# Cross-attention with layer norm: first input block in rows of 2 KB, keys by input block, third tile's transpose later

## The chip, the cores and the metric

The kernel runs on one core of a Trainium2 chip. The metric is the device time of one execution in microseconds (us). The runs of the kernel before give a median of 541.96 us.

The names of the engines are those of the profile: PE is TensorE (matmuls; PEld its weight loads), DVE is VectorE, ACT is ScalarE, POOL is GpSimd, and SP is SyncE, which here only issues DMAs.

## The reference, cut to what matters

Sixteen heads of 32 channels attend from 4 x 2048 rows of `x` (512 channels) to 77 rows of context per batch. The result goes through an output projection, the input is added, and a layer norm follows.

```python
qs = (q @ wq)   # q = x, split into 16 heads of 32
ks = (k @ wk)   # k = ctx_1024, 77 rows per batch
vs = (v @ wv)   # v = ctx_1024
scores = einsum('bhqd,bhkd->bhqk', qs, ks) / sqrt(32)
scores = where(mask, -inf, scores)
attn = einsum('bhqk,bhkd->bhqd', softmax(scores), vs)
out = attn.reshape(B, L, 512) @ wo + q
return (out - mean(out)) / sqrt(var(out) + 1e-5) * gamma + beta
```

## The kernel before

**Tiles, blocks and groups.** The 8192 rows are cut into 64 tiles of 128 rows. Two tiles make a block (32 blocks), and four tiles a group (16 groups), which is what one load of the transposed input `xT` brings. Every projection is done in three matmuls per 128 input channels: each operand is split into a rounded part and a rest (ACT copies the rounded part, DVE or POOL subtracts), and rounded x rounded, rounded x rest and rest x rounded are added up in PSUM. The 512 input channels are four such input blocks, called c = 0 to 3 below.

**What one tile goes through.**

- `q_visit` (L154): the query projection, one quarter of the output channels of a group at a time, into one PSUM bank; `q_evac` (L171) copies it to SBUF on DVE.
- `scores` (L277): 16 small matmuls into four PSUM banks.
- `maxima` (L291): 16 DVE instructions, which add the mask, take the row maximum and write the scores to `pbuf[t % 3]`. The first four heads empty the first bank, and so on.
- `exps` (L305): 16 ACT instructions. `recip` (L316) on DVE, then `normalise` (L321) on POOL.
- `transp` (L345): DVE transposes the 128 x 1280 probabilities in 32 x 32 squares into the tile `B`, of which one holds the two tiles of a block.
- `regroup` (L357): when both tiles of a block are transposed, SP issues 12 DMAs, which carry `B` to `PT`.
- `av` (L375): attention x values, for a block; `av_hi` (ACT, L406) and `av_lo` (DVE, L410) split the result; `o_proj` (L430) is the output projection; then residual, moments and scale.

**Order.** Nothing is reordered by a scheduler: each engine runs its instructions in the order in which the program issues them. A loop runs over u = 0, 2, 4, ... and issues the work of tiles u and u + 1 together with older stages of earlier tiles; the last 16 tiles follow a list written out by hand (`ORDER`), which the change doesn't touch. Two PSUM facts matter: there are eight banks in all, and a matmul into a new bank waits until the bank's last reader is done.

**The buffer of B.** `B` has two buffers. At the start they hold `ctx_f` and `ctx_h` (the context and its rounded part). `B_0` (tiles 0 and 1) takes the place of `ctx_f`. `ctx_h` is read until the value projections of batches 2 and 3 (L215, issued at u = 4), so `B_1` (tiles 2 and 3) takes the buffer of `B_0`. The first transpose into `B_1`, `transp(2)`, therefore waits until all 12 DMAs of `regroup(0)` have read `B_0`. In the loop body of u = 2 it is issued after `maxima(3)` and `values_evac`, and ahead of `split_wo(2)`, `split_wo(3)` (L246), `recip(3)` and, in the body of u = 4, `maxima(4)`.

**The start.** Ten matmuls on a zero tile (L499, `pw`) keep PE busy from the first microsecond. Meanwhile SP issues in turn a quarter of the first 256 rows of `xT` (128 KB in rows of 1 KB, L507) and a quarter of `wq` (256 KB in rows of 2 KB, L508), four times; then the context (L510), `wk` (L512, loaded into `stage_a` and split into `woh` and `wol`, whose buffers serve `wo` later), the mask, and the second 256 rows of the group (L515). Eight semaphores go round over SP's DMAs, so that a DMA is issued only when the one eight places before it has landed. For each c, ACT and DVE split the piece of `xT` and of `wq` (L125, L126) and PE runs 12 matmuls for tiles 0 and 1 (L523). Then the keys follow (L180), into four banks, one for each quarter m of the output channels:

```python
for m in range(NG):
    keys_part(pks, m, (0, 1))
for m in range(NG):
    keys_part(pks, m, (2, 3))
```

`keys_part(pks, m, cs)` runs three matmuls for each c of `cs`: with `woh`, with `woh` and the context's rest, and with `wol`. So the first quarter asks for c = 1 after three matmuls. Behind the keys come `q_visit(0, 0)` for the second 256 rows and `scores(0)`.

Of the kernel before, what the change touches and what calls it, by code (L numbers as in the profile page):

```python
# [17 lines left out]
P = 128  # L18
# [9 lines left out]
NG = H // GH  # L28
HEADS = [GH * g + j for j in range(GH) for g in range(NG)]
NC_D = D // P  # L30
BLK = 256
GRP = 2 * BLK
MASKED = -3.0e38
EPS = 1.0e-5
WARM = 10
NPB = 3
LAST = 16

# [24 lines left out]
def xattn_layernorm(  # L63
    ctx: ExitStack,
    tc: tile.TileContext,
    x: bass.AP,
    xT: bass.AP,
    ctxT: bass.AP,
    mask: bass.AP,
    wq: bass.AP,  # L70
# [7 lines left out]
    nc = tc.nc  # L78
# [10 lines left out]
    def bank(name):  # L89
        return ps.tile([P, 512], F32, tag="mm", name=name)  # L90
# [20 lines left out]
    stage_a = sb.tile([P, 2, NC_D, D], F32, tag="PT", name="stage_a")  # L111
# [9 lines left out]
    def wview(w, c):  # L121
        return w[c * P : (c + 1) * P, :]

    def split(hi, lo, src):
        nc.scalar.copy(hi, src)  # L125
        nc.vector.tensor_tensor(lo, src, hi.bitcast(F32), ALU.subtract)  # L126
# [4 lines left out]
    fx, gx, qd, qp, bat, pts = {}, {}, {}, {}, {}, {}  # L131
# [44 lines left out]
    def keys_part(pks, m, cs):  # L176
        for c in cs:
            n = 0
            for w, i in ((woh, 0), (woh, 1), (wol, 0)):
                nc.tensor.matmul(  # L180
                    pks[m][:, : NB * (NK + 1)],
                    w[:, c, m * P : (m + 1) * P],
                    ctx_s[c][i][:, :, : NK + 1],
                    start=(c == 0 and n == 0),
                    stop=(c == NC_D - 1 and n == 2),
                )
                n += 1
# [12 lines left out]
    def value_rows():  # L200
        vi = sb.tile([NK2, 2, 32], F32, tag="o", bufs=8, name="vi")
        for q0 in range(0, NK2, 32):
            for a, (z0, z1) in enumerate(((NK, NK2), (NK - TAIL_K, NK))):
                nc.vector.memset(vi[q0 : q0 + 32, a], 1.0)
                lo, hi = max(z0, q0), min(z1, q0 + 32)
                if lo < hi:
                    nc.vector.memset(vi[q0 : q0 + 32, a, lo - q0 : hi - q0], 0.0)
        nc.vector.transpose(vm, vi)
# [128 lines left out]
    def transp(t):  # L337
        b, tt = divmod(t, 2)
        if tt == 0:
            bts[b] = sb.tile([P, 5, 2 * NP * 32], F32, tag="B", name=f"B_{b}")  # L340
        if b < NBLK - 1:
            bt = bts[b].rearrange("p c (q t r) -> p c q t r", q=NP, t=2)[:, :, :, tt, :]
        else:
            bt = bts[b].rearrange("p c (t q r) -> p c q t r", q=NP, t=2)[:, :, :, tt, :]
        nc.vector.transpose(  # L345
            bt.rearrange("p c q r -> p q c r"),
            pbuf[t % NPB].rearrange("p q (c r) -> p q c r", c=5),
        )
# [92 lines left out]
    def moments(t):  # L441
        b, tt = divmod(t, 2)
        st = sb.tile([P, 6], F32, tag="st", bufs=3, name=f"st_{t}")
        nc.vector.bn_stats(st, od[t])
        if tt == 0:
            mvs[b] = sb.tile([P, 2, 2], F32, tag="mv", bufs=3, name=f"mv_{b}")
            rns[b] = sb.tile([P, 2, 2], F32, tag="rn", bufs=3, name=f"rn_{b}")
        mv, rn = mvs[b], rns[b]
        nc.vector.bn_aggr(mv[:, tt, :], st)
        nz = bat[t // TPB][1]  # L450
        if tt == 1:
            k = (t - 1) % TPB
            nc.gpsimd.tensor_tensor(rn[:, 0, :], mv[:, :, 1], nz[:, k : k + 2], ALU.add)
            nc.gpsimd.tensor_tensor(rn[:, 0, :], rn[:, 0, :], mhalf, ALU.pow)
            nc.gpsimd.tensor_tensor(rn[:, 1, :], mv[:, :, 0], rn[:, 0, :], ALU.mult)
            nc.gpsimd.tensor_tensor(rn[:, 1, :], rn[:, 1, :], mneg, ALU.mult)
# [40 lines left out]
    pw = bank("pw")  # L497
    for i in range(WARM):
        nc.tensor.matmul(pw, warm[:, :P], warm, start=True, stop=True)  # L499
# [3 lines left out]
    gx[0] = [sb.tile([P, NC_D, GRP], F32R, tag=t, name=f"{t}_0") for t in ("xth", "xtl")]  # L503
    qd[0] = sb.tile([P, NG, GRP], F32, tag="q", name="q_0")
    x0h, x0l = (a[:, :, :BLK] for a in gx[0])
    for c in range(NC_D):
        nc.sync.dma_start(fx[0, c // 2 * 2][:, c % 2, :BLK], xT[0, :, c, :BLK])  # L507
        nc.sync.dma_start(stage_a[:, 0, c], wview(wq, c))  # L508
    for c in range(0, NC_D, 2):
        nc.sync.dma_start(ctx_f[:, c : c + 2], ctxT[:, c : c + 2])  # L510
    for c in range(NC_D):
        nc.sync.dma_start(stage_a[:, 1, c], wview(wk, c))  # L512
    load_mask(0)
    for c in range(0, NC_D, 2):
        nc.sync.dma_start(fx[0, c][:, :, BLK:], xT[0, :, c : c + 2, BLK:])  # L515
    value_rows()
    pq0 = [bank(f"pq_0_{m}") for m in range(NG)]
    for c in range(NC_D):
        split(x0h[:, c], x0l[:, c], fx[0, c // 2 * 2][:, c % 2, :BLK])
        split(wqh[:, c], wql[:, c], stage_a[:, 0, c])  # L520
        for m in range(NG):
            for n, (w, r) in enumerate(((wqh, x0h), (wqh, x0l), (wql, x0h))):
                nc.tensor.matmul(  # L523
                    pq0[m][:, :BLK],
                    w[:, c, m * P : (m + 1) * P],
                    r[:, c, :],
                    start=(c == 0 and n == 0),
                    stop=(c == NC_D - 1 and n == 2),
                )
# [4 lines left out]
        nc.scalar.copy(qd[0][:, m, :BLK], pq0[m][:, :BLK])  # L534
        nc.vector.tensor_copy(qd[0][:, m + 1, :BLK], pq0[m + 1][:, :BLK])
    pks = [bank(f"pk_{m}") for m in range(NG)]
    for m in range(NG):
        keys_part(pks, m, (0, 1))
    for m in range(NG):
        keys_part(pks, m, (2, 3))  # L540
    for c in range(0, NC_D, 2):
        split(*(a[:, c : c + 2, BLK:] for a in gx[0]), fx[0, c][:, :, BLK:])
    q_visit(0, 0)
    mask_bias(0, slice(0, 1))
    gate(stage_a[:, 1, NC_D - 1, D - 1 :])
# [17 lines left out]
    def pieces(u):  # L563
        return casts.get(u) or [((u + 8) // 4, u % 4)] * (u + 8 < 4 * NGRP)

    evac = [(0, 0)]
    for u in range(0, NT - LAST // 2, 2):
        n = u // 2
        m, k = divmod(u, TPB)

        for q in pieces(u + 2):
            if u >= 4:
                load_xT(*q)
        for t in (u - 4, u - 3):
            if t >= 0:
                load_x(t)
        scores(u)
        maxima(u, 0, H // 2)
        for q in evac:
            q_evac(*q)  # L580
        maxima(u, H // 2, H)
        for q in pieces(u):
            cast_xT(*q)
        exps(u, 0, 3 * H // 4)
        for v in list(vd):
            values_evac(v)
        for q in pieces(u):
            split_xT(*q)
        if u == 0:
            mask_bias(0, slice(1, TPB))  # L590
            split_wv()
        if u >= 6:
            o_proj(u - 6)
        for v in {2: (0,), 4: (2, 3)}.get(u, ()):
            values(v)
        for q in visits(u):
            q_visit(*q)
        if u >= 6:
            residual(u - 6)
            moments(u - 6)  # L600
        if u:
            transp(u - 1)
            regroup(n - 1)
        if u >= 8:
            scale(u - 8)
            scale(u - 7)
        exps(u, 3 * H // 4, H)
        if u >= 8:
            affine(u - 8)
        for q in visits(u):  # L610
            q_evac(*q)
        if u == 0:
            load_wo()
            nc.gpsimd.memset(ident, 0.0)
            nc.gpsimd.affine_select(ident, ident, [[-1, P]], ALU.not_equal, 1.0, base=0, channel_multiplier=1)
        if u == 2:
            split_wo(0)
            split_wo(1)
        if k == TPB - 6 and m + 1 < NB:
            load_mask(m + 1)  # L620
        if k == TPB - 4 and m + 1 < NB:
            mask_bias(m + 1)
        if k == TPB - 2 and m + 1 < NB:
            mask_nan(m + 1)

        scores(u + 1)
        maxima(u + 1, 0, 3 * H // 4)
        recip(u)
        maxima(u + 1, 3 * H // 4, H)
        exps(u + 1, 0, H // 4)  # L630
        normalise(u)
        if u >= 8:
            affine(u - 7)
        for v in list(vd):
            values_evac(v)
        if u >= 4:
            av(n - 2)
            av_hi(n - 2, 0)
            av_hi(n - 2, 1)
        exps(u + 1, H // 4, H)  # L640
        if u >= 5:
            o_proj(u - 5)
        if u >= 4:
            av_lo(n - 2, 0)
        if u >= 5:
            residual(u - 5)
        if u >= 4:
            av_lo(n - 2, 1)
        transp(u)
        for v in {2: (1,)}.get(u, ()):  # L650
            values(v)
        evac = visits(u + 1)
        for q in evac:
            q_visit(*q)
        if u == 2:
            load_xT(*pieces(4)[0])
        if u >= 5:
            moments(u - 5)
        if u == 0:
            mask_nan(0)  # L660
        if u == 2:
            split_wo(2)
            split_wo(3)
        recip(u + 1)
        normalise(u + 1)
        if u >= 8:
            store(u - 8)
            store(u - 7)
# [79 lines left out]
```

## Time and profile before

| | us |
|---|---|
| median of 3 runs | 541.96 |
| lowest and highest run | 539.43, 542.49 |
| the profiled execution | 540.23 |
| its span (first to last instruction) | 538.5 |
| PE busy in the span | 522.8 |
| DVE, ACT, POOL busy | 483.6, 462.6, 404.5 |

The profiled execution took 540.23 us, that is 1.73 us less than the median and inside the spread of the runs; 1.7 us of it lie outside the span. Places in time below are us from the start of the span. In a timeline a row has its start, its duration, engine, line, operation, output<-inputs and shape; in square brackets stands how long the engine had been idle before it and what ended that. In the chain of waits a row is a start, a duration and what the end of the span was waiting for in that time. A list of waits gives the total, how many times and the longest. Matmuls are pipelined, so that rows overlap: a 256-column matmul of the start has a row of 0.28 us, but the next one starts 0.12 us after it.

### The profile page before, as it was taken

To read this page: it belongs to the slowest core of one execution; us is meant where nothing else is said; L and a number is where in the kernel's file an instruction comes from. 1 tells how busy PE (TensorE), PEld (TensorE's weight loads), DVE (VectorE), ACT (ScalarE), POOL (GpSimd) and SP (SyncE) were. 2 spreads that over 40 slices of the span, in tenths; PEclk is the share of its full clock that TensorE was granted. 3 is DMA by queue.
4 is the path that set the end of the run, shared out by engine and by line. 5 is a ranking of instruction groups with operands and counts; after the bars stand their busy time and mean duration, and the time that the engine had idled before them with its cause. 6 is when DMAs were issued, how large, how long until landed. Compare 5 with 4: busy or idle time off the path is not lost.

```text
span 538.5 us, 16101 instructions
## 1 busy us (share of the span) xinstructions
PE 522.8 (97%) x4810; PEld 398.9 (74%) x4810; DVE 483.6 (90%) x2588; ACT 462.6 (86%) x2217; POOL 404.5 (75%) x367
## 2 busy tenths in 40 slices
PE   8999899999999999999999999999999999999795
PEld 5987577777777777777777778777777777766573
DVE  5688899889999898889998998889999988999977
ACT  5687799998899999998899999998899998998410
POOL 0626447888899888888899888888899888856851
PEclk9999999999999999999999999999999999999998
DMA  8934577787777787886777778867777767855854
GB/s 279 401 134 107 160 200 193 211 238 189 191 195 210 214 226 208 225 221 175 193 210 221 209 217 218 235 167 198 210 208 217 216 175 197 236 138 158 255 157 156
DMA packets 59191, 109.96 MB, mean 204 GB/s; under 512 B 9424, under 2 KB 11920, under 8 KB 59104
## 3 DMA queue, kind: packets, MB, share of 16 engines
q1 hardware_dynamic: 56048, 103.10, 68.3%
q0 software_dynamic: 2256, 5.05, 3.4%
q8 instruction: 38, 0.62, 0.5%
q10 hardware_dynamic: 800, 0.79, 0.5%
q14 instruction: 49, 0.40, 0.3%
HBM read 41.79 MB, written 16.78 MB: 109 GB/s over the span
## 4 chain that ended last, share of the span: by engine, by line
PE 76%; DVE 13%; DMA 4%; SPq 2%; ACT 2%; issue 1%; POOL 1%; DVEq 0%; ACTq 0%
PE po L430 29%; PE pq L154 26%; PE sc L277 10%; PE pa L375 9%; DVE pbuf L291 4%; DVE B L345 3%; DMA PT<-B 3%; SPq L357 1%; ACT pbuf L305 1%; PE pk L180 1%; DMA stage_a<-wk 1%; DVE o L486 1%; DVE q L171 1%; DVE AL L410 1%; DVE o L489 1%
## 5 line engine op out<-in xcount | busy, mean ns | idle before, releaser
L305 ACT ACTIVATE pbuf<-pbuf,nm 128x77 f32<-128x77 f32 x1024 | 355.0, 371 | 32.4 <-DVE nm L291 31.1
L305 ACT ACTIVATION_READ_ACCUMULATOR pbuf<-pbuf,nm 128x1 f32 x1024 | 216.4, 211 | 0.0
L321 POOL TENSOR_TENSOR pbuf<-pbuf,ri 128x1232 f32<-128x1232 f32 x63 | 142.3, 2259 | 56.0 <-DVE ri L316 37.2
L291 DVE CUSTOM_DVE_ANT_0 pbuf<-sc,mb 128x77 f32<-128x77 f32 x1024 | 169.2, 231 | 5.5 <-PE sc L277 3.6
L430 PE MATMUL po<-woh,AH 128*128 128x512 f32 x256 | 107.8, 421 | 1.5 <-DVE nm L291 1.5
L345 DVE STREAM_TRANSPOSE B<-pbuf 128x1280 f32<-128x1280 f32 x64 | 95.6, 1494 | 6.5 <-DMA PT<-B 3.5
L430 PE MATMUL po<-wol,AH 128*128 128x512 f32 x256 | 100.3, 392 | 0.0
L430 PE MATMUL po<-woh,AL 128*128 128x512 f32 x256 | 100.1, 391 | 0.0
L154 PE MATMUL pq<-xth,wqh 128*128 128x512 f32 (+1 forms) x256 | 98.6, 385 | 1.4 <-DVE nm L291 1.4
L154 PE MATMUL pq<-xtl,wqh 128*128 128x512 f32 (+1 forms) x256 | 97.9, 383 | 0.0
L154 PE MATMUL pq<-xth,wql 128*128 128x512 f32 (+1 forms) x256 | 97.8, 382 | 0.0
L291 DVE DVE_READ_ACCUMULATOR2_ANT nm<- 128x1 f32 x1024 | 84.7, 83 | 0.0
L277 PEld LDWEIGHTS sc<-kct,q 32*128 32x128 f32 x2048 | 62.8, 186 | 21.9 <-issue 14.1
L277 PE MATMUL sc<-kct,q 32*128 32x77 f32 x2048 | 72.1, 277 | 0.0
L467 POOL TENSOR_TENSOR o<-o,bet 128x512 f32<-128x512 f32 x50 | 65.7, 1314 | 3.9
L147 POOL TENSOR_TENSOR xtl<-xtf,xth 128x1024 fp32r<-128x1024 f32 x28 | 67.1, 2399 | 0.0
L430 PEld LDWEIGHTS po<-woh,AH 128*128 128x128 f32 x256 | 48.0, 188 | 24.0 <-DVE nm L291 8.1
L466 POOL TENSOR_TENSOR o<-o,gam 128x512 f32<-128x512 f32 x50 | 64.3, 1286 | 0.2
L375 PE MATMUL pa<-PT,vsb 96*32 96x256 f32 x992 | 60.2, 382 | 3.0 <-DMA PT<-B 2.8
L439 DVE TENSOR_TENSOR o<-po,o 128x512 f32<-128x512 f32 x56 | 38.5, 687 | 22.4 <-PE po L430 22.2
L154 PEld LDWEIGHTS pq<-xth,wqh 128*128 128x128 f32 x256 | 48.1, 188 | 12.0 <-DVE nm L291 2.5
L430 PEld LDWEIGHTS po<-woh,AL 128*128 128x128 f32 x256 | 48.1, 188 | 10.7
(99 smaller groups left out, 672.3 us busy)
## 6 DMA issues: line engine op xcount, KB each, us to landing
PT<-B SPq DMA_DIRECT2D x352, 128.0 KB, 2.4
o<-x SPq DMA_DIRECT2D x64, 256.0 KB, 4.9
out<-o SPq DMA_DIRECT2D x64, 256.0 KB, 2.9
xtf<-xT SPq DMA_DIRECT2D x28, 512.0 KB, 5.1
PT<-B POOLq DMA_DIRECT2D x18, 128.0 KB, 4.7
stage_a<-wq SPq DMA_DIRECT2D x4, 256.0 KB, 4.2
stage_a<-wk SPq DMA_DIRECT2D x4, 256.0 KB, 6.3
stage_b<-wv SPq DMA_DIRECT2D x4, 256.0 KB, 5.0
```

Of the source, the lines that this page charges most:

```text
L147: nc.gpsimd.tensor_tensor(l, fx.pop((g, c)), h.bitcast(F32), ALU.subtract)
L154: nc.tensor.matmul(pq, w[:, c, m * P : (m + 1) * P], r[:, c, rs], start=(n == 0), stop=(n == 11))
L277: nc.tensor.matmul(sc[j][:, g * NK : (g + 1) * NK], qs[q, g, rs], kct[q, g, t // TPB, keys_of(j)], start=True, stop=True,)
L291: nc.vector.tensor_tensor_reduce(pb[:, h // 2, (h % 2) * NK : (h % 2 + 1) * NK], scs[t][j][:, g * NK : (g + 1) * NK], mb[:, t % TPB, keys_ ...
L305: nc.scalar.activation(pb[:, h // 2, (h % 2) * NK : (h % 2 + 1) * NK], pb[:, h // 2, (h % 2) * NK : (h % 2 + 1) * NK], AF.Exp, bias=nmax[t ...
L321: nc.gpsimd.tensor_tensor(pv, pv, rv.to_broadcast((P, NP, 2, NK)), ALU.mult)
L345: nc.vector.transpose(bt.rearrange("p c q r -> p q c r"), pbuf[t % NPB].rearrange("p q (c r) -> p q c r", c=5),)
L375: nc.tensor.matmul(pas[b, g // 2][HD * j : HD * (j + 1), (g % 2) * BLK : (g % 2 + 1) * BLK], vsb[:, 2 * b // TPB, HD * h : HD * (h + 1)], ...
L430: nc.tensor.matmul(pos[t], a[:, c, rs], w[:, c, :], start=(first and c == 0 and n == 0), stop=(c == NC_D - 1 and n == 2),)
L439: nc.vector.tensor_tensor(od[t], pos.pop(t), od[t], ALU.add)
L466: nc.gpsimd.tensor_tensor(o, o, gam, ALU.mult)
L467: nc.gpsimd.tensor_tensor(o, o, bet, ALU.add)
```

## The change

The change has four edits, all of which concern the first 65 us.

- The first group of `xT` comes from a second copy of those rows, `xT0`, laid out by halves of 256 rows. Two input blocks (c, c + 1) come in one DMA of 256 KB with rows of 2 KB, so two DMAs stand where four stood; the order on SP is now x (c = 0, 1), `wq` 0, `wq` 1, x (c = 2, 3), `wq` 2, `wq` 3. The second half of the rows comes in two DMAs as before, also in rows of 2 KB where there were two rows of 1 KB.
- There are nine of the matmuls on the zero tile, where there were ten.
- The keys run by input block: for each c, all four quarters m.
- `transp(2)` is issued in the body of u = 4, after `maxima(4)` and directly ahead of `transp(3)`, instead of in the body of u = 2.

```diff
-WARM = 10
+WARM = 9
...
-    for c in range(NC_D):
-        nc.sync.dma_start(fx[0, c // 2 * 2][:, c % 2, :BLK], xT[0, :, c, :BLK])
+    f0 = {c: fx[0, c].rearrange("p c r -> p (c r)").rearrange("p (h c r) -> p h c r", h=2, c=2) for c in (0, 2)}
+    for c in range(0, NC_D, 2):
+        nc.sync.dma_start(f0[c][:, 0], xT0[0, :, c : c + 2])
         nc.sync.dma_start(stage_a[:, 0, c], wview(wq, c))
+        nc.sync.dma_start(stage_a[:, 0, c + 1], wview(wq, c + 1))
...
     for c in range(0, NC_D, 2):
-        nc.sync.dma_start(fx[0, c][:, :, BLK:], xT[0, :, c : c + 2, BLK:])
+        nc.sync.dma_start(f0[c][:, 1], xT0[1, :, c : c + 2])
...
-        split(x0h[:, c], x0l[:, c], fx[0, c // 2 * 2][:, c % 2, :BLK])
+        split(x0h[:, c], x0l[:, c], f0[c // 2 * 2][:, 0, c % 2])
...
-    for m in range(NG):
-        keys_part(pks, m, (0, 1))
-    for m in range(NG):
-        keys_part(pks, m, (2, 3))
+    for c in range(NC_D):
+        for m in range(NG):
+            keys_part(pks, m, (c,))
     for c in range(0, NC_D, 2):
-        split(*(a[:, c : c + 2, BLK:] for a in gx[0]), fx[0, c][:, :, BLK:])
+        split(*(a[:, c : c + 2, BLK:] for a in gx[0]), f0[c][:, 1])
...
+        if u == 4:
+            transp(2)
         if u:
             transp(u - 1)
             regroup(n - 1)
...
-        transp(u)
+        if u != 2:
+            transp(u)
...
+        "xT0": np.ascontiguousarray(xf[:GRP].reshape(2, BLK, Dm // P, P).transpose(0, 3, 2, 1)),
```

More of the change, by code (lines that the diff above doesn't have):

```diff
@@ L67, in xattn_layernorm @@
     xT: bass.AP,
+    xT0: bass.AP,
     ctxT: bass.AP,
```

## The prediction

> **What bounds the kernel now.** I read the page's engine totals first, then the chain of waits in three windows, then the list of PE's waits.
>
> ```profile
> PE 522.8 (97%) x4810; PEld 398.9 (74%) x4810; DVE 483.6 (90%) x2588; ACT 462.6 (86%) x2217; POOL 404.5 (75%) x367
> by line: PE po L430 38.8%; PE pq L154 35.2%; PE sc L277 14.1%; PE pa L375 12.1%
> ```
>
> PE is busy for 97% of the span. The second line is the chain from 130 to 300 us: PE alone. The chain from 58 to 130 us is PE alone from 64.13 us on. So whatever PE gains before 64 us should reach the end, and whatever another engine gains counts only where PE waits for it. PE's waits in the first 62 us are these, behind the first 1.2 us:
>
> ```profile
> PE pq L154 <- DVE nm L291: 1.4, 1, 1.4
> PE pk L180 <- DVE wol L126: 0.4, 2, 0.2
> PE pk L180 <- ACT woh L125: 0.3, 1, 0.3
> PE pq L523 <- DVE wql L126: 0.2, 1, 0.2
> ```
>
> The first is the largest. The timelines of DVE and PE show where it comes from:
>
> ```profile
> 51.02 0.86 DVE L222 TENSOR_SCALAR vsb<-pv,small 96x256 f32<-96x256 f32 x2
> 55.38 1.51 DVE L345 STREAM_TRANSPOSE B<-pbuf 128x1280 f32<-128x1280 f32 x1 [3.49 <-DMA PT<-B]
> 56.81 1.25 DVE L246 TENSOR_TENSOR wol<-stage_b,woh 128x512 fp32r<-128x512 f32 x2
> 58.86 0.50 PE L154 MATMUL pq<-xth,wqh 128*128 128x512 f32 x1 [1.42 <-DVE nm L291]
> 64.13 1.07 PE L375 MATMUL pa<-PT,vsb 96*32 96x256 f32 x16 [0.20 <-DVE q L171]
> ```
>
> DVE stands 3.49 us ahead of transp(2), until regroup(0) has read the buffer. Behind it queue the two `split_wo`, recip(3) and maxima(4), whose first four heads free the bank that `q_visit(2, 1)` needs at 57.44 us.
>
> **Edit 1: transp(2) behind maxima(4).** DVE is free at 51.88 us. The two `split_wo` take 1.18, to 53.06. recip(3) then waits for the last exponential of tile 3, which ACT ends at 54.33; with 0.2 us for itself, maxima(4) starts at about 54.55 instead of 58.14. Its first bank is free at 55.25, ahead of the 57.44 at which PE asks. PE gets the 1.42 us.
>
> What is late next? DVE: eight maxima (1.27), a copy of q (0.60), eight maxima (1.27) and the values' copies (0.79) bring 58.5; transp(2), with nothing to wait for since `regroup(0)` landed at 55.2, and transp(3) follow at 1.42 each, to 61.3; the copy of q ends at 61.9. transp(3) needs normalise(3) on POOL: 54.55 + 2.26 = 56.8, in time. Before, that copy ended at 64.0, so DVE is 2.1 us ahead here, with a transpose more behind it. PE: `q_visit(2, 1)` ends at 60.4, scores(5) at 61.5, and the second half of av(0) wants its bank at 62.5, which the copy frees at 61.9. So the 0.20 us goes too. SP starts `regroup(1)` at 61.4 instead of 63.53, which is early by more than av(1) is.
>
> ACT gains least. Its cast for group 3 starts at 56.98, because that load stands on SP behind the 12 DMAs of `regroup(0)`; nothing there changes. exps(4) then starts at 58.0 instead of 58.42, and exps(5) at 63.45 instead of 64.33: 0.9 us. Through recip(5), which waits for exps(5), DVE has only these 0.9 us at maxima(6) (70.2 instead of 71.10), while PE is 1.62 ahead. PE's scores(7), at 74.84 before, moves to 73.2; the two banks of maxima(6) that it needs are free at about 73.0 before and 72.1 after. Later DVE itself waits for PE (1.13 us idle ahead of the residual at 96.19), so the difference is made up. Sum: 1.42 + 0.20 = **1.62 us**. If the 0.9 us bound PE it would be 0.9; that is the lower end.
>
> **Edit 2: keys by input block.**
>
> ```profile
> 12.35 0.42 PE L180 MATMUL pk<-ctx_h,woh 128*128 128x312 f32 x1 [0.34 <-ACT woh L125]
> 13.07 0.42 PE L180 MATMUL pk<-ctx_h,wol 128*128 128x312 f32 x1 [0.16 <-DVE wol L126]
> 14.14 0.42 PE L180 MATMUL pk<-ctx_h,wol 128*128 128x312 f32 x1 [0.19 <-DVE wol L126]
> ```
>
> The idle times here are after modelled ends; the starts tell more. A key matmul starts 0.147 us after another when nothing waits, and 0.26 behind one that waited. Before, the sixth one waits until 14.14 for `wol` of c = 1. Now the fourth to the twelfth use c = 0 alone: they run from 13.33, the thirteenth comes at 14.65, and the fifteenth asks at 14.95 for the `wol` that is there at 14.09. c = 2 and 3 are asked for at 16.4 and 18.2 and stand ready at 15.2 and 16.2. The 48th starts at 13.33 + 44 x 0.147 = 19.80, and the next projection at 19.93 instead of 20.56: **0.63 us**. The third matmul's wait (13.07) stays. All four banks now end late, the last at 20.1; its copy to `kct` (0.62 on DVE) is done by 20.8, and the 24 matmuls of `q_visit(0, 0)` (2.96 us) cover it, since scores(0) starts at 22.9. Without that cover it would cost 0.6.
>
> **Edit 3: two transfers of 2 KB rows, nine warm-up matmuls.** The bytes are the same. Here the trace has no row of the new transfer, so both ends:
>
> ```profile
> DMA packets 194, 0.24 MB, mean 240 GB/s; under 512 B 22, under 2 KB 132, under 8 KB 194
> DMA packets 385, 0.38 MB, mean 382 GB/s; under 512 B 23, under 2 KB 380, under 8 KB 385
> ```
>
> These are the DMA counts of 5 to 6 us, where pieces of x and `wq` mix, and of 13 to 14 us, where the second half of x comes in rows of 1 KB. From 15 to 16 us, all rows of 2 KB, it is 406 GB/s. By the second row 1 KB costs 6% against 2 KB: on 512 KB of x, 0.1 us. By the first, a packet took 16 engines x 1.04 us / 194 = 86 ns whatever its size; 256 packets less on 16 engines are 1.4 us. Against that, 256 KB instead of 128 KB now stand ahead of `wq` 0, which then lands some 0.4 us later than at 4.06; but PE is bound further on, by `wq` 2, `wq` 3 and `wk` 0 (cast at 7.71, 8.88 and 11.67). The delay of the first matmul, from about 5.2 to 5.5, is absorbed there: the waits at 7.31 and 9.11 have it to spare. So from 0 to 1.4 us at the start of the keys, passed on whole as the keys wait for `wk` (PE's queries end at 11.85). I take **0.6 us**, a little under the middle, as the row of the same 1 KB packets weighs more than the row of the same time. SP has two issues of 0.47 us less ahead of `wk`, which is worth nothing by itself: `wk` 0 landed 6.2 us after its issue. The later loads gain as little, and nothing waits for them.
>
> [...]
>
> The removed warm-up matmul ends nothing on the path:
>
> ```profile
> L499 PE MATMUL pw<-ident x10: 393/634/634, 1.2 to 5.0; 128*128 128x512 bf16 x10
> ```
>
> Nine lasted 634 ns as modelled, 0.43 us apart, and the tenth, at 5.0 us, 393 ns: PE became fast at about 5.0 us, after 3.8 us of work, with nine matmuls done. Nine now end at the same 5.0 us. Term: 0.
>
> [...]
>
> **Sum.** 1.62 + 0.63 + 0.6 = 2.85 us. The profiled execution took 540.23, so it would take 537.4. It lies 1.73 below the median of 541.96; from the median the forecast is **539.1 us**, 0.53% less. What a measurement of this kernel can tell from no change is about 0.5%, 2.7 us, so the forecast stands just beyond it.
>
> **The rivals.**
>
> *The transfers bring nothing.* For it: 382 GB/s in rows of 1 KB. Against: the eight pieces took from 3.20 to 8.88 us, 1.4 MB at 250 GB/s, so something other than bytes is slow there. Then 1.62 + 0.63, and at most 0.3: 2.25 to 2.55, or 539.4 to 539.7, within 0.5%.
>
> *ACT becomes the bound behind tile 4.* Its 0.9 us instead of 1.62, for instance if scores(7) needs more of maxima(6) than I think: 0.9 + 0.63 + 0.6 = 2.1, or 539.8. Against: the slack of 0.9 us worked out above, and DVE's idle times at 96 us.
>
> *Slower: PE stays slow behind the ninth warm-up matmul.* The place is 5.0 to 5.5 us, where PE now idles until `wqh` 0 is there. If the idle time makes PE miss the step that came at 5.0, each query matmul starts 0.22 instead of 0.12 us after the last (zero matmuls 0.43 apart, 512-column ones 0.23 apart at 29 us). Through the whole query block, 48 x 0.22 from 5.4 ends at 16.0; the keys then end at 23.0 instead of 20.56, +2.5, less 1.62: 542.8. Through the keys too, 48 x 0.12 more: 548.6. It decides from about 40 slow matmuls, that is if PE is still slow at 14 us. Against: the profile shows the step before the tenth matmul, and short waits at 7.31 and 9.11 didn't undo it.
>
> **How the numbers follow.** The forecast, with 0.45 to 1.4 us from the transfers, 538.3 to 539.25: 0.55. Transfers worth nothing: 0.30. ACT binds: 0.10, also within 0.5%. PE slow through the keys, which alone is over 0.5% slower: 0.05. Range: the lower bound of the sum is 541.96 - 1.62 - 0.63 - 1.4 = 538.3, the upper, with 0.9 and no gain from the transfers, 540.4. The runs before lie up to 2.5 us from each other and their median, so I add 0.9 us on either side: 537.4 to 541.3. That leaves out most of the slow case.
>
> **What would show each step.** The wait of 3.49 us ahead of a transpose should be gone and PE's 1.42 at `q_visit(2, 1)` with it; a transpose pair should stand on DVE behind maxima(4). There should be one wait for `wol` in the keys, and 6.7 us from the third key matmul to `q_visit(0, 0)`. The cast of `wk` 0 should start at about 11.1; at 11.6 the transfers brought nothing. PE's first scores should come at about 22.3 instead of 23.52, and those of tile 7 some 2.8 us before 74.84. If the scores come early and the end doesn't, the gain was lost behind 64 us, which would make the prediction wrong.

## The result, and the profile after

The changed kernel takes 539.85 us (median of 20 runs, 535.52 to 541.79); the kernel before, in 20 runs beside it, 542.83 (539.43 to 545.03). The ratio is 0.9934, with an interval of 0.9912 to 0.9955: 2.98 us less, and by the interval 2.4 to 4.8. The forecast was 539.1, faster.

The profiled execution took 540.01 us (span 538.2), only 0.22 less than the 540.23 of before. Its start and its end therefore tell different things, and I read the start first. Engine totals of the page and the shares of the chain over the whole span, after the change:

```profile
PE 525.2 (98%) x4809; PEld 400.9 (74%) x4809; DVE 484.2 (90%) x2588; ACT 463.5 (86%) x2217; POOL 404.4 (75%) x367
PE 86%; DVE 7%; DMA 4%; SPq 1%; ACT 1%; issue 1%; POOL 0%; DVEq 0%; ACTq 0%
```

PE had 76% of the chain before and DVE 13%. PE's list of waits from 0 to 62 us is now one line, the start itself; the four waits shown of before are gone from it (the list leaves out a short one in the keys, which the starts below show):

```profile
PE pw L500 <- DVE ident L493: 1.2, 1, 1.2
```

DVE's timeline after the change (start, duration, engine, line, operation; every line number is one to three higher than before):

```profile
50.60 2.21 DVE L247 TENSOR_TENSOR wol<-stage_b,woh 128x512 fp32r<-128x512 f32 x2
53.17 0.25 DVE L317 RECIPROCAL ri<-sum 128x16 f32<-128x16 f32 x1 [0.36 <-ACT pbuf L306]
53.34 0.19 DVE L292 CUSTOM_DVE_ANT_0 pbuf<-sc,mb 128x77 f32<-128x77 f32 x1
...
57.21 2.89 DVE L346 STREAM_TRANSPOSE B<-pbuf 128x1280 f32<-128x1280 f32 x2
```

The 3.49 us in front of a transpose are gone. recip(3) waits 0.36 us for ACT, maxima(4) follow at 53.34, and both transposes stand behind them without a pause. PE's timeline at that place, first before (two rows not shown yet), then after:

```profile
57.04 0.40 PE L215 MATMUL pv<-wvh,ctx_lAL 128*96 128x512 f32 x1
59.19 0.40 PE L154 MATMUL pq<-xtl,wqh 128*128 128x512 f32 x1
```

```profile
55.84 0.40 PE L216 MATMUL pv<-wvh,ctx_lAL 128*96 128x512 f32 x1
56.07 0.39 PE L155 MATMUL pq<-xth,wqh 128*128 128x512 f32 x1
56.30 0.39 PE L155 MATMUL pq<-xtl,wqh 128*128 128x512 f32 x1
```

Before, 2.15 us passed from the last value matmul (57.04) to the second query matmul (59.19); now 0.46 (55.84 to 56.30). That is 1.69, not 1.42. The weighted values of block 0 (av), first before (the row of their second half stands in the prediction), then after:

```profile
62.86 1.07 PE L375 MATMUL pa<-PT,vsb 96*32 96x256 f32 x16
65.13 0.50 PE L154 MATMUL pq<-xth,wqh 128*128 128x512 f32 x1
```

```profile
59.95 1.93 PE L376 MATMUL pa<-PT,vsb 96*32 96x256 f32 x32
61.81 0.50 PE L155 MATMUL pq<-xth,wqh 128*128 128x512 f32 x1
```

From their first matmul to the next query matmul 2.27 us passed before and 1.86 after: 0.41, not 0.20. The cast of `wk` 0 on ACT, before and after, is where the loads of the start show:

```profile
11.67 0.62 ACT L125 CAST woh<-stage_a 128x512 fp32r<-128x512 f32 x1 [1.07 <-DMA stage_a<-wk]
11.10 0.62 ACT L126 CAST woh<-stage_a 128x512 fp32r<-128x512 f32 x1 [1.12 <-DMA stage_a<-wk]
```

It starts 0.57 us earlier. The first query matmul behind the keys before, and then the keys in the new order:

```profile
20.56 0.28 PE L154 MATMUL pq<-xth,wqh 128*128 128x256 f32 x1
```

```profile
12.04 0.31 PE L181 MATMUL pk<-ctx_h,woh 128*128 128x312 f32 x1
12.18 0.31 PE L181 MATMUL pk<-ctx_lAH,woh 128*128 128x312 f32 x1
12.50 0.42 PE L181 MATMUL pk<-ctx_h,wol 128*128 128x312 f32 x1
12.76 0.31 PE L181 MATMUL pk<-ctx_h,woh 128*128 128x312 f32 x1
...
19.36 0.28 PE L155 MATMUL pq<-xth,wqh 128*128 128x256 f32 x1
...
22.32 0.91 PE L278 MATMUL sc<-kct,q 32*128 32x77 f32 x24
```

One pause, ahead of the third matmul, and 6.86 us from there to the first query matmul behind the keys (7.49 before, 13.07 to 20.56): 0.63.

PE's scores, by the start of their first matmul:

| tile | before | after | earlier by |
| --- | --- | --- | --- |
| 0 | 23.52 | 22.32 | 1.20 |
| 5 | 61.80 | 58.88 | 2.92 |
| 6 | 68.08 | 64.76 | 3.32 |
| 20 | 175.46 | 172.15 | 3.31 |
| 57 | 455.26 | 451.94 | 3.32 |

So 3.3 us are gained by 65 us and kept to PE's last scores, which start at 487.54 instead of 490.87. All but 0.3 us of it (the spans are 538.5 and 538.2) are lost behind them in this execution. The windows of 5 us, after the change (busy time of PE, PEld, DVE, ACT, POOL with counts; then granted clock, DMA share, GB/s):

```profile
505.00:510.00 5.00, 2.50 (x30) 1.52 (x32) 3.37 (x7) 0.59 (x1) 4.55 (x9) 0.84 0.83 254
510.00:515.00 5.00, 5.00 (x19) 2.67 (x12) 3.31 (x5) 0.59 (x1) 2.60 (x6) 0.50 0.80 193
515.00:520.00 5.00, 5.00 (x23) 4.14 (x22) 3.12 (x6) 0.00 (x0) 1.17 (x2) 0.98 0.50 173
```

and before:

```profile
510.00:515.00 5.00, 3.56 (x38) 2.20 (x39) 3.33 (x5) 1.17 (x2) 4.48 (x11) 1.00 0.76 236
515.00:520.00 5.00, 5.00 (x24) 4.12 (x23) 4.45 (x9) 0.00 (x0) 2.11 (x4) 1.00 0.77 225
```

The clock that PE was granted fell to one half for some 6.8 us in the execution after (1.6 in the first window, 5.0 in the second, 0.2 in the third), and did not while PE worked in the one before. It fell behind an idle time of PE in which the weighted values wait for a regrouping DMA:

```profile
507.81 3.13 PE L376 MATMUL pa<-PT,vsb 96*32 96x256 f32 x32 [2.50 <-DMA PT<-B]
```

These 32 matmuls take 1.93 us at full clock. Both kernels have executions whose mean granted clock is lower and such in which it isn't, and the time follows it. Of the changed kernel's 20 runs, 5 with 0.995 or more lie at 535.5 to 537.3, 3 with 0.993 at 537.8 to 538.5, 9 with 0.991 at 539.3 to 540.5, 3 with 0.987 to 0.990 at 541.0 to 541.8.

### The profile page after: what moved, and what is told of

Its sections match the earlier page's. It is cut to its first block, busy times and chain, and to the rows that moved or that the text cites. A ratio compares the mean times of both kernels' runs of the same rounds, so it can differ in the third digit from the quotient of the medians.

```text
span 538.2 us, 16096 instructions
## 1 busy us (share of the span) xinstructions
PE 525.2 (98%) x4809; PEld 400.9 (74%) x4809; DVE 484.2 (90%) x2588; ACT 463.5 (86%) x2217; POOL 404.4 (75%) x367
## 4 chain that ended last, share of the span: by engine, by line
PE 86%; DVE 7%; DMA 4%; SPq 1%; ACT 1%; issue 1%; POOL 0%; DVEq 0%; ACTq 0%
PE pq L155 31%; PE po L431 30%; PE sc L278 11%; PE pa L376 10%; DMA PT<-B 3%; PE pv L216 2%; DVE B L346 2%; DVE pbuf L292 1%; PE pk L181 1%; DVE o L487 1%; DMA stage_a<-wq 1%; SPq L358 1%; DVE AL L411 1%; DVE o L490 1%; DVE st L476 1%
## 5 line engine op out<-in xcount | busy, mean ns | idle before, releaser
L306 ACT ACTIVATION_READ_ACCUMULATOR pbuf<-pbuf,nm 128x1 f32 x1024 | 207.8, 203 | 0.0
L292 DVE DVE_READ_ACCUMULATOR2_ANT nm<- 128x1 f32 x1024 | 85.8, 84 | 0.0
L431 PEld LDWEIGHTS po<-wol,AH 128*128 128x128 f32 x256 | 48.4, 189 | 9.8 <-issue 1.5
```

Source lines behind the costliest of these rows:

```text
L292: nc.vector.tensor_tensor_reduce(pb[:, h // 2, (h % 2) * NK : (h % 2 + 1) * NK], scs[t][j][:, g * NK : (g + 1) * NK], mb[:, t % TPB, keys_ ...
L306: nc.scalar.activation(pb[:, h // 2, (h % 2) * NK : (h % 2 + 1) * NK], pb[:, h // 2, (h % 2) * NK : (h % 2 + 1) * NK], AF.Exp, bias=nmax[t ...
L431: nc.tensor.matmul(pos[t], a[:, c, rs], w[:, c, :], start=(first and c == 0 and n == 0), stop=(c == NC_D - 1 and n == 2),)
```

## The experiments

All medians are of the experiment's own chip, beside the kernel before on it. "Cast to scores" is the time from the cast of `wk` 0 (ACT) to tile 0's first scores; "scores 0 to 6" is from tile 0's first scores to tile 6's.

**The transpose alone** (kernel before, with the move):

```diff
+        if u == 4:
+            transp(2)
...
-        transp(u)
+        if u != 2:
+            transp(u)
```

> The kernel before with edit 1 alone (transp(2) behind maxima(4)). Place to read: the start of the scores of tile 0 (before 23.52, changed kernel 22.32) and of tile 6 (before 68.08, changed kernel 64.76). Theory (the wait for the buffer of B cost PE 2.1 us, read by starts of matmuls: 1.69 at the query projection and 0.41 in av(0)): tile 0 stays at 23.5, tile 6 comes at 66.0, time 2.1 us less, 0.4%. The recorded sum said 1.62, so 66.5. Rival (the gain depends on the earlier start, because ACT binds behind tile 4): tile 6 at 67 or later.

Measured: 540.0 us against 543.78, ratio 0.9936 (0.9909 to 0.9964). Tile 0's scores came at 22.94 and tile 6's at 65.39, both earlier than expected because the cast of `wk` 0 came at 11.09 in this execution; the stretch between them is what the move is read by. Scores 0 to 6 take 42.45 us instead of 44.56: 2.11. In the ten profiles with the move this stretch is 42.43 to 42.49 us; in the four without it, 44.18 to 45.25. So the move is worth 1.7 to 2.8 us and brings the most of the whole. The rival did not come: the stretch is the same 42.44 us where the first scores came as late as 23.47 and 23.77 (rows of 1 KB, and no warm-up, below). The measured ratio alone says 2.0 to 4.9 us, which is too wide to weigh 1.62 against 2.1; the trace does that.

**The keys alone** (kernel before, with the new loop over c):

```diff
-    for m in range(NG):
-        keys_part(pks, m, (0, 1))
-    for m in range(NG):
-        keys_part(pks, m, (2, 3))
+    for c in range(NC_D):
+        for m in range(NG):
+            keys_part(pks, m, (c,))
```

> The kernel before with edit 2 alone (keys by input block). Theory: the 48 key matmuls lose the second wait for wol, 0.63 us; scores of tile 0 at 22.89 and, since the wait for the buffer of B moves along with the start, scores of tile 6 at 67.45. Rival (the second wait comes back at another input block, or the copies of the keys, now all late, hold the scores): tile 0 at 23.2 or later.

Measured: 542.32 us (one run). Tile 0's scores came at 22.60 and tile 6's at 67.07, against 22.89 and 67.45 expected; the cast came at 11.39 here and not at 11.67. From the third to the last key matmul 6.71 us, where before had 7.35. Cast to scores 11.21, as in the changed kernel (11.22) and in three more profiles with this order; the four with the old order and ten warm-up matmuls have 11.83 to 11.85. That is 0.62 to 0.64 us.

**The transfers alone** (kernel before, with all new loads of `xT0`, those of the second half of the rows too; cut to the first half):

```diff
-    for c in range(NC_D):
-        nc.sync.dma_start(fx[0, c // 2 * 2][:, c % 2, :BLK], xT[0, :, c, :BLK])
+    for c in range(0, NC_D, 2):
+        nc.sync.dma_start(f0[c][:, 0], xT0[0, :, c : c + 2])
...
```

> The kernel before with the new transfers of edit 3 alone, ten warm-up matmuls and the old order of the keys. Theory (the transfers bring the first piece of wk 0.57 us earlier and that is passed on whole): cast of that piece at 11.1 instead of 11.67, scores of tile 0 at 22.95. Rival 1 (the 0.57 us of the changed kernel's one profile are chance of the early loads): the cast lies anywhere from 11.1 to 11.7. Rival 2 (the old order of the keys waits for the second piece of wk and swallows it): cast at 11.1, scores at 23.3 or later.

Measured: 540.89 us (one run), cast of `wk` 0 at 11.22, cast to scores 11.83. But the transpose alone, with the old transfers, had that cast at 11.09. One pair of profiles does not price this edit; the samples are put together below.

**The changed kernel with ten warm-up matmuls:**

```diff
-WARM = 9
+WARM = 10
```

> The changed kernel with ten warm-up matmuls instead of nine. In the changed kernel's profile the first six real matmuls came 0.21 us apart and only from 6.66 on 0.12. Theory (the number of warm-up matmuls changes nothing on the path, as the keys wait for wk): scores of tile 0 at 22.3 to 22.4 whenever PE becomes fast. Rival (the ninth to tenth matmul decides whether PE becomes fast at 5.0 or at 6.6, and that is on the path): fast at 5.0 and scores of tile 0 at 21.9 or earlier.

Measured: 535.51 us (one run). The cast came at 10.77, the first scores at 21.98: 11.21 behind it, as with nine. PE became fast at 6.15 here, so the rival's condition (fast at 5.0) did not arise. The tenth matmul bought nothing in this run; the time is low because the clock stayed at 1.00 to PE's last matmul.

**Two transfers, but rows of 1 KB:**

```diff
-        nc.sync.dma_start(f0[c][:, 0], xT0[0, :, c : c + 2])
+        nc.sync.dma_start(f0[c][:, 0], xT[0, :, c : c + 2, :BLK])
```

> The changed kernel, but its two first-half transfers of x read rows of 1 KB instead of 2 KB, so number and order of the transfers are the new ones and the row size is the old one. Theory (it is the rows): the cast of wk 0 comes later than in the changed kernel's profile, at 11.4 to 11.7 us instead of 11.10. Rival (it is the number and order of the transfers): 10.8 to 11.2. Second rival (the early loads vary from execution to execution by as much as the edit is worth): anywhere from 10.8 to 11.7; the five profiles besides before's have 10.77 to 11.39. In every case the first scores follow 11.2 us behind that cast, as in the changed kernel (22.32 - 11.10) and in the runs with the new order of the keys.

Measured: 538.02 us (one run), cast at 11.49. The first scores came 11.98 us behind it and not 11.2: a miss, and the reason is PE. Its timeline in this run:

```profile
9.58 0.41 PE L526 MATMUL pq<-xth,wql 128*128 128x256 f32 x1
9.79 0.37 PE L526 MATMUL pq<-xth,wqh 128*128 128x256 f32 x1
10.00 0.28 PE L526 MATMUL pq<-xtl,wqh 128*128 128x256 f32 x1
10.12 0.28 PE L526 MATMUL pq<-xth,wql 128*128 128x256 f32 x1
```

Up to 10.00 the query matmuls start 0.21 us apart, from there on 0.12 (9.79 is the start of the last slow one). The granted clock of the windows from 0 to 10 us reads 1.00 in the profiles before and after, slow matmuls or not, so the slow stretch at the start is read from the distance of the starts alone. In the changed kernel's profile this step is at 6.66:

```profile
6.45 0.36 PE L526 MATMUL pq<-xth,wql 128*128 128x256 f32 x1
6.66 0.28 PE L526 MATMUL pq<-xth,wqh 128*128 128x256 f32 x1
6.77 0.28 PE L526 MATMUL pq<-xtl,wqh 128*128 128x256 f32 x1
```

In the run with rows of 1 KB the first query matmul came late, at 5.48, some 0.5 us behind the ninth warm-up matmul (which starts at 4.58; they start 0.43 us apart, so a tenth would have come at 5.01). The slow stretch made the way from the cast to the scores 11.98 - 11.21 = 0.77 us longer. This is the prediction's slower rival at its place, at a third of its price.

**Second sample of these rows, with ten warm-up matmuls:**

```diff
-        nc.sync.dma_start(f0[c][:, 0], xT0[0, :, c : c + 2])
+        nc.sync.dma_start(f0[c][:, 0], xT[0, :, c : c + 2, :BLK])
...
-WARM = 9
+WARM = 10
```

> Second sample of the two transfers in rows of 1 KB, now with ten warm-up matmuls. So far the cast of wk 0 came at 11.67, 11.09 and 11.39 us with the old transfers (mean 11.38), at 11.10, 11.22, 10.77, 10.80, 10.37 and 10.55 with the new ones (mean 10.80), and at 11.49 with two transfers of 1 KB rows. Theory (the rows are what the edit gains by): 11.2 to 11.7. Rival (number and order of the transfers): 10.4 to 11.1. PE should become fast earlier than the 9.79 us of the run with nine warm-up matmuls if the pause of 0.26 us behind the ninth was what kept it slow.

Measured: 536.72 us (one run), cast at 11.58, PE fast by 5.98, cast to scores 11.21. The cast of `wk` 0 over all profiles:

| transfers | cast of `wk` 0 at | mean |
| --- | --- | --- |
| four, 1 KB rows | 11.67, 11.09, 11.39, 11.84 | 11.50 |
| two, 1 KB rows | 11.49, 11.58 | 11.54 |
| two, 2 KB rows | 11.10, 11.22, 10.77, 10.80, 10.37, 10.55, 10.97, 11.51 | 10.91 |

The means of the first and the last row differ by 0.59 us, though the values overlap, and two transfers with the old rows look like the old ones. That speaks for the rows and against number and order; two samples are few for it. These two keep the rows of 2 KB for the second half, so that half is not what the edit gains by. The extremes of the last row, 10.37 and 11.51, have no and twelve warm-up matmuls; its five profiles with nine or ten have a mean of 10.92. On each chip the mean of the rows of 2 KB is the lower one, by 0.2 to 0.9 us.

**Five warm-up matmuls, and none**, each in a kernel of its own:

```diff
-WARM = 9
+WARM = 5
```

```diff
-WARM = 9
+WARM = 0
```

> The changed kernel with 5 warm-up matmuls instead of 9: PE stands idle from about 3.3 to 4.9 us. Theory (PE becomes fast some 3.8 us of work after it starts afresh, and the waits for the weights absorb most of the slow part): query matmuls 0.21 to 0.22 us apart until about 8.7, the last one at 12.2 to 12.5 instead of 11.92, the third key matmul 0 to 0.5 us later than the 12.50 of the changed kernel, the first scores 11.2 to 11.6 us behind the cast of wk 0. Rival (the slower one of the prediction): PE stays slow through the whole query block, whose last matmul then comes at about 16, and the scores 3 us or more later. Second rival (nothing is lost, the work done before the idle time counts): last query matmul at 11.9.

> The changed kernel without any warm-up matmul. If idle time of 1.6 us undoes what the warm-up did, this run starts like the one with five: fast from about 8.7 us, scores 11.2 to 11.6 us behind the cast of wk 0. If the work before the idle time counts, this one is later than the one with five by 0.2 to 0.6 us. The prediction's slower rival gives a last query matmul at about 16 and scores over 3 us later.

Measured: with five, fast from 9.81, last query matmul 13.04, cast to scores 12.36; with none, fast from 11.03, 13.65 and 13.40. Both expectations of when PE becomes fast (8.7) and what it costs (up to 0.4) were too low: from the first query matmul (5.12 and 5.25) the slow stretch lasted 4.7 and 5.8 us, and the way from the cast to the scores is longer than 11.21 by 1.15 and 2.2 us. Part of that is the cast, which came early here (10.80 and 10.37): the scores themselves came at 23.16 and 23.77, that is 0.8 and 1.5 us behind the changed kernel's 22.32. The rival's 16 us did not come either. The times, 538.10 and 537.63 (one run each), are below the changed kernel's median, as neither profile has the fall of the clock behind 505 us: single times say nothing about the start of this kernel.

**The low parts of the weights last:**

```diff
-        for m in range(NG):
-            keys_part(pks, m, (c,))
+        for ns in ((0, 1), (2,)):
+            for m in range(NG):
+                keys_part(pks, m, (c,), ns)
```

(and the same for the first queries).

> The changed kernel, but within each input block the matmuls that need the low part of a weight (wql, wol) run behind those that need the high part, for the first queries and for the keys. Theory: the third key matmul no longer waits for wol 0, so the keys run without a pause from their first to their last matmul: 47 x 0.147 = 6.9 us instead of 7.17, and the first scores 10.9 to 11.0 us behind the cast of wk 0 instead of 11.2. Time: 0.2 to 0.3 us under the changed kernel's, ratio to before 0.993, which a measurement can't tell from the changed kernel's. Rival: the pause moves to another input block or to the queries' end, and the scores stay 11.2 us behind the cast.

Measured: 538.24 us against 543.18, ratio 0.9923 (0.9894 to 0.9951). The pause ahead of the third key matmul is gone, but cast to scores is 11.29: the rival held. The cast came early (10.55) and PE was slow for its first eight real matmuls, so the queries' end set the keys.

**Filling PE's idle time at the end** (six matmuls into the bank that `av` overwrites):

```diff
+        for _ in range(FILL * (b == NBLK - LAST // 2 + 6)):
+            nc.tensor.matmul(pas[b, 0], warm[:, :P], warm, start=True, stop=True)
```

> The changed kernel with six matmuls of zeros and ones, whose result is overwritten, put ahead of the weighted values (av) of the second last block of four full heads groups, where PE stands idle from about 505.1 to 507.8 us. In the ten profiles so far the granted clock fell to 0.50 behind that idle time in four of the seven with 2.5 us or more of it and in none of the three with 1.47 to 1.99 us. Theory (that idle time triggers the fall): with six matmuls of 0.215 us the idle time shrinks to 0.2 to 1.7 us, the clock stays 1.00 to PE's last matmul, the span is 533.5 to 535 us, and the median of the time 535.5 to 536.5 us instead of 539.85; the runs lie within about 2 us of each other. Rival (the fall has another cause, the load or the time since the start): clock 0.5 somewhere from 505 to 520 us again in about every second run, median 539 to 540, spread 6 us as before.

Measured: 537.25 us against 543.44, ratio 0.9901 (0.9864 to 0.9938). Seven of eight runs lie at 536.81 to 537.75, each with a clock of 0.995 or more; one, with 0.991, took 540.61. PE's row and the window in this run's profile:

```profile
507.91 1.93 PE L379 MATMUL pa<-PT,vsb 96*32 96x256 f32 x32 [0.83 <-DMA PT<-B]
510.00:515.00 5.00, 5.00 (x21) 3.77 (x21) 4.36 (x7) 0.49 (x1) 3.05 (x7) 1.00 0.86 241
```

With 0.83 us of idle time left the clock stays. The median is 0.75 us above the range that I gave, but the cause holds: without the filling 15 of 20 runs were under 0.995, with it one of 8, and none of 6 in the last experiment.

**The same filling, with the same two lines, in the kernel before:**

> The kernel before with the same six matmuls ahead of the same av. Theory (the idle time triggers the fall): no fall of the clock, median 538.5 to 540 us instead of 542 to 543.5. Together with the changed kernel's version of it on the same chip this prices the change without the clock: it should be faster than this one by what the first scores and the maxima behind tile 4 gave in the profiles, 3.0 to 3.6 us, and not by 2.85 as forecast. Rival: median 542 to 543, as before.

Measured: 541.58 us, ratio 0.9975 (0.9950 to 1.0001); 6 of 12 runs are still under 0.995. The profile, of one of these six, shows why:

```profile
512.87 3.21 PE L378 MATMUL pa<-PT,vsb 96*32 96x256 f32 x32 [2.08 <-DMA PT<-B]
515.00:520.00 5.00, 5.00 (x19) 2.68 (x12) 3.36 (x5) 0.64 (x2) 1.79 (x4) 0.50 0.65 174
```

Here the DMA came so late that six matmuls left 2.08 us idle, and the clock fell. So 2.5 us is no bound: over all profiles falls came with 2.08, 2.50, 2.50, 2.94 and 3.00 us, none with 2.58, 2.61 and 2.82, nor with anything up to 2.00; what separates them is not shown. Among the runs with a clock of 0.995 or more, the two filled kernels have medians of 540.30 (6 runs, 539.15 to 542.11) and 537.18 (7 runs, 536.81 to 537.75): with the clock out of it they differ by 3.1 us, where the trace shows 3.3.

**All together:** the low parts last and the filling as above, and

```diff
-WARM = 9
+WARM = 12
```

> All together: the changed kernel with the low parts of the weights last within each input block, six filling matmuls ahead of that av, and 12 warm-up matmuls instead of 9, so that PE works without a pause into the first query. Theory: PE becomes fast between 4.8 and 7.5 us and not as late as the 9.79 of the run with rows of 1 KB, the first scores come 11.0 to 11.2 us behind the cast of wk 0, no fall of the clock at the end; median 0.2 to 0.5 us under the changed kernel with the filling alone, about 535.3 to 536. Rival: the three warm-up matmuls more delay the first queries by up to 1.3 us where the step comes late, and the median is the same or later than with the filling alone.

Measured: 536.05 us against 543.44, ratio 0.9888 (0.9849 to 0.9927), the lowest median of the kernels with more than one run, and all six runs have a clock of 0.995 or more. Cast to scores is 10.77, better than the 11.0 to 11.2 expected, and PE is fast by 6.37. The 1.2 us to the filling alone lie within the intervals, and the profile shows less: its scores of tile 6 come at 64.72 against 64.67, because the cast of `wk` 0 came late (11.51).

## Why the prediction was right, and where it was not

**Edit 1: right in mechanism, mis-sized.** The term was 1.42 + 0.20 = 1.62; the runs show 2.1. Its step "PE gets the 1.42 us" took the idle time of the row, which counts from the modelled end of the matmul before. Start to start the first wait was 1.59 and the slower restart behind it 0.10; the other 0.4 lie at av(0), booked at 0.20. The same text said for the keys that "the starts tell more", and then didn't apply it here. The scores of tile 7 came 3.3 us earlier (71.53), where 2.8 was expected.

**ACT as the bound: refuted.** recip(5) does wait 1.25 us for ACT at 68.75, as worked out, and maxima(6) gain from it what was said: they start at 68.92 instead of 71.10, of which 1.20 are the start's and 0.98 the move's (0.9 forecast). But the lead of PE stays at 3.32 us from tile 6 to tile 57. The slack held.

**Edit 2: right.** 0.63 forecast, 0.63 in the first pair of profiles and 0.62 to 0.64 from the cast to the scores. The sign that the prediction gives for it, 6.7 us from the third key matmul to the next projection, doesn't follow from its own sum (19.93 - 13.07 = 6.86), and 6.86 is what came. The copy to `kct` is covered, as PE goes from the queries to the scores without a wait.

**Edit 3: right in size, on thinner ground than it looked.** 0.6 forecast, 0.57 in the first pair, 0.59 between the means. But the cast moves by up to 1.1 us between executions of equal loads (0.7 among those with nine or ten warm-up matmuls), more than the term; the forecast of 11.1 could have missed with the step right. Rows of 1 KB had the cast at 11.51 on average (six profiles), rows of 2 KB at 10.91 (eight), with the scatter just named.

**The warm-up term: 0 was luck in part.** "PE became fast at about 5.0 us" was one sample; the step came between 4.8 and 7.1 us in the runs with nine to twelve, and at 10.00 in one with nine. In the changed kernel's own profile six query matmuls ran slow and the wait for `wk` took it up. The rival gave about 40 slow matmuls as what decides; a cost that a term of 0 leaves out starts far below, as 19 of them already cost 0.77 us. Whether the pause behind the ninth or the moment alone makes the step so late, no run settles, as none changes only that; the profiles compared in the last section speak for the pause.

**The sum.** 2.1 + 0.63 + 0.57 = 3.3 in the trace against 2.85 forecast; 2.98 between the medians. The median of before rose from 541.96 (3 runs) to 542.83 (20), so that 539.85 lies 0.75 above the forecast of 539.1 although the gain is 0.13 larger than forecast. That the medians agree so well is luck in part: the interval allows 2.4 to 4.8 us, and the term of edit 1 was 0.5 too small. The prediction's test "if the scores come early and the end doesn't, the gain was lost behind 64 us" came true in the profiled execution, though not in the medians: the loss is the clock at the end, which the prediction didn't name. The page of before held the hint, the 2.82 us in front of the same `av`.

## What to carry to other kernels

Price a wait by the starts of the matmuls around it, with its neighbours' undisturbed spacing subtracted, and add the slower restart; the idle time in the row came out a quarter too small here. Before pricing an edit of some tenths at the start, ask how far that point moves between executions of the same loads. When two profiles differ in their middle and agree at their end, look at the granted clock by windows before looking for a new wait.

## What the runs showed that I had not expected

PE lost clock in most executions of these two kernels: 36 of 45 runs of the kernel before beside the experiments, and 15 of 20 of the changed one, have a mean clock under 0.995. Where it is lost is known from the profiles alone: five of the 14 have a fall before PE's last matmul, all five at this `av`. These five have a mean clock of 0.991 to 0.993, the other nine 0.996 to 0.999. The times stand in steps of about 1.9 us (medians of 536.2, 538.2, 540.1 and 541.8 for 0.995 and more, 0.993, 0.991, and 0.987 to 0.990). Here the clock fell in or behind modelled idle times of 2.1 to 3.0 us, though not with three of 2.6 to 2.8; in the two filled versions of the changed kernel, with 0.83 and 1.11 us left, it stayed at 1.00 to PE's last matmul.

The falls differ from profile to profile. After the change the clock was at one half from 508.38 to 515.21, which is 6.83 us, and again from 535.69 on (behind PE's last matmul). By the windows of 5 us, the falls with the transpose alone (0.89, 0.50, 0.93), with the keys alone (0.98, 0.50, 0.83) and in the filled kernel before (0.84, 0.50, 0.98) lasted 6.8 to 6.9 us too; with the transfers alone (0.66 in one window) it was 3.4. As an estimate, PE loses half of such a stretch: 1.7 us of the 3.4, in the one profile with 0.993, and 3.4 of the 6.8, in the four with 0.991. That is near one and two of the steps seen. Nor is the moment the same. With the transpose alone and the keys alone the clock fell at about 508.9 and 509.8, inside idle times that ended at 509.36 and 510.63; after the change and in the filled kernel before, at 508.38 and about 513.4, 0.5 to 0.6 us behind their end. Why the idle time of 2.08 us came with a fall and those of 2.58, 2.61 and 2.82 did not is not shown: no run moved an idle time alone.

In the profiles of the changed kernel, of its filled version and of the rows of 1 KB, all with nine warm-up matmuls, the first query matmul came at 4.92, 5.26 and 5.48. The query matmuls start 0.12 us apart from 6.66 in the first and from 6.77 in the second, but only from 10.00 in the third. With these rows and ten warm-up matmuls the first query matmul came later still, at 5.72, 0.08 us behind the modelled end of the tenth, and PE was fast by 5.98.
